# A four-layer graph network on one core: node blocks handed to the next layer while edge sums still run, four-step windows, node sums on TensorE

## The chip, the cores and the metric

The kernel runs on 1 core of one Trainium2 chip. The metric is device time in microseconds (us), and the time of a kernel is the median of its runs. A separate execution was taken with the hardware profiler; its own time is given beside the span of its trace.

## The reference

There are 6250 nodes with 128 features, 100000 edges sorted by destination, and four layers. Each layer gives a new value per node that is added to x and normalised over its 128 features. What each layer computes, cut to the sums over edges:

```
# layer 0, two rounds: attention with self loops (h = x @ W_node + b first)
g = h @ W;  e = leaky_relu((g*a_src).sum(-1)[src] + (g*a_dst).sum(-1)[dst], 0.2)
ex = exp(e - segment_max(e, dst)[dst])
h = segment_sum(g[src] * (ex / segment_sum(ex, dst)[dst]), dst) + bias
# layer 1: convolution with weights and degrees (deg: sums of weights plus 1)
out = segment_sum((x @ W)[src] * dis[src] * w * dis[dst], dst) + b
# layer 2: messages from x[src], edge type and time; 8-head attention over dst
message = x[src] * rel_emb * sigmoid(relu([x[src], rel_emb, time] @ W1 + b1) @ W2 + b2)
scores = ((x[dst] @ Wq + bq) * (message @ Wk + bk)).sum per head / 4
out = segment_sum((message @ Wv + bv) * softmax over dst (scores), dst)
# layer 3: gated recurrent update from summed messages
agg = segment_sum((h @ W_msg)[src], dst);  out = GRU(agg, h) @ W_out.T + b_out
# after each layer
x = layernorm(x + out)
```

The destinations are drawn as the square of a uniform number times 6250, so low node numbers have many more edges than high ones.

## The kernel before

The nodes are 49 blocks of 128, taken in 13 batches of up to 4 blocks (GROUPS). The edges are cut so that each of 832 steps (K) holds at most 128 edges that all go to one block. The steps follow the blocks in order, so the sums of low blocks are complete while later steps are still running.

The program is a row of stages. Where the text says "edge stage", the 832 steps are run in groups of 16 (U). For one step an indirect DMA issued by GpSimd (gather, L133) fetches the 128 source rows of a node table that the stage before has written to DRAM. A 128x128 matrix of zeros and ones (sel, written once to DRAM by the first stage and read back by SyncE in groups of 1 MB) says which row goes to which node of the block. One TensorE matmul adds sel-transposed times rows into PSUM (L415). The edge stages are attention 0 and 1 (attention_edges), the convolution and the messages of layer 3 (sum_edges), the scores of layer 2, and the weighted values of layer 2, which read rows that the scores stage has stored and so have no gathers.

The PSUM places are kept by the class Windows. A window is M = 8 steps. It opens three PSUM banks with three matmuls of zeros (L412), its eight steps add into places of 136 columns picked by a register, then one identity matmul adds what the first block of the window had before (L422), and ScalarE copies all nine places to the sums in SBUF, ACC (L431). The registers are loaded per group on TensorE and ScalarE.

An attention stage works in chunks of T = 64 steps, which is four groups. The destination terms are spread to the edges by matmuls with row selections (rsel, made on VectorE from dlrow, a row that a DMA spreads over the partitions, L382). When all 64 steps' rows are there, VectorE adds the last column of the gathered rows (L477, one operation per group), makes e (L479), scans for the running maximum over each destination (L485 to L505), and prepares shrink (L520, L522), which scales the sums of the chunk before. Only then are the rows scaled on ScalarE and summed. The gathered rows thus stay in their buffers (g, seven of one group in attention, eight in sum_edges) until that is done.

Between the edge stages lie node stages. They run over the 13 batches with all of the engines but GpSimd: they finish the sums (merged, or the lines after sum_edges), add to X (in SBUF for all 49 blocks), take means and variances on VectorE (stats), normalise everything when the last batch has its statistics (normalize, L342), and then make the next stage's table (for example attention_tables) and write it to DRAM. The next stage's gathers start when the table is written. After the last stage X is written to the output by two DMAs.

The order of instructions on each engine is set by a scheduler that follows the program's order and data[...].

Of the kernel before, what the change touches and what calls it, by code (L numbers as in the profile page):

```python
# [9 lines left out]
F32 = mybir.dt.float32  # L10
# [10 lines left out]
P = 128  # L21
# [13 lines left out]
M = 8  # L35
SB = 3
BANK = 512
SB_TOP = M // SB * BANK + M % SB * W
U = 16
T = 64  # L40
# [9 lines left out]
def kernel(ctx: ExitStack, tc: tile.TileContext, a: dict, out: bass.AP):  # L50
# [36 lines left out]
    Mt = table("mt", NP, D)  # L87

# [32 lines left out]
    MV = const.tile([P, NB, 2], F32, name="MV")  # L121
    VE = const.tile([P, NB], F32, name="VE")
    RS = const.tile([P, NB], F32, name="RS")
    NEWTON = const.tile([P, NB], F32, name="NEWTON")
# [122 lines left out]


# [45 lines left out]
    Wx, bl = [], []  # L294
    for l in range(2):
        w = const.tile([D, 130], F32, name=f"Wx{l}")
        nc.sync.dma_start(w[:, 0:D], a["L0_gnn_lyr_W"][l])
        Wx.append(w)
        bl.append(load(f"bl{l}", row_bcast(a["L0_gnn_lyr_bias"][l], D), P, D))
    W1l = load("W1l", a["L1_gnn_W"], D, D)  # L300
    b1l = load("b1l", row_bcast(a["L1_gnn_b"], D), P, D)
# [10 lines left out]


    def transposed(work, psum, src, g, name):
        pt = psum.tile([P, B, P], F32, name="tr", bufs=2)
# [6 lines left out]
    def stats(work, t0, g):  # L322
        for t in range(t0, t0 + g):
            s6 = work.tile([P, 6], F32, name="s6")
            nc.vector.bn_stats(s6, X[:, t, :])
            nc.vector.bn_aggr(MV[:, t, :], s6)

    def inverse_root(r, v):

        nc.scalar.activation(r, v, AF.Sqrt)  # L330
        nc.vector.reciprocal(r, r)
        for _ in range(2):
            nc.vector.tensor_mul(NEWTON, r, r)
            nc.vector.tensor_mul(NEWTON, NEWTON, v)
            nc.vector.tensor_scalar(NEWTON, NEWTON, -0.5, 1.5, op0=OP.mult, op1=OP.add)
            nc.vector.tensor_mul(r, r, NEWTON)

    def normalize():
        nc.vector.tensor_scalar(VE, MV[:, :, 1], EPS, None, op0=OP.add)
        inverse_root(RS, VE)  # L340
        for t in range(NB):
            nc.vector.tensor_scalar(X[:, t, :], X[:, t, :], MV[:, t, 0:1], RS[:, t:t + 1],  # L342
                                    op0=OP.subtract, op1=OP.mult)

    def by_step(keep, work, psum, rows, name):
# [3 lines left out]
        for k0 in range(0, K, K // 2):  # L349
            pv = psum.tile([P, K // 2], F32, name="bs", bufs=1)  # L350
# [22 lines left out]
    def row_selections(work, k0, make=False, n=U):  # L373
# [3 lines left out]
        if make:  # L377
            for h in range(2):
                n = U * P // 2
                row = work.tile([P, n], BF16, name="dlrow")  # L380
# [7 lines left out]
    class Windows:  # L388
# [4 lines left out]
        def __init__(self, psum, k0):  # L393
# [752 lines left out]
```

## Time and profile before

| | |
|---|---|
| Timed, median of 3 | 8493.26 us (8485.22 to 8526.25) |
| Profiled execution | 6808.89 us, span of its trace 6807.1 us |
| Granted TensorE clock, mean | 0.678 |
| PE, PEld, DVE, ACT, POOL busy | 62%, 44%, 26%, 33%, 62% |

The profiled execution is 1684 us shorter than the timed runs.

The stages, read from GpSimd's gathers and the matmuls of the windows, in us from the span's start:

| stage | from | to |
|---|---|---|
| preparation, first node stage | 0 | 140 |
| attention 0 | 140 | 1186 |
| node stage | 1186 | 1304 |
| attention 1 | 1304 | 2354 |
| node stage | 2354 | 2495 |
| convolution | 2495 | 3534 |
| node stage, queries | 3534 | 3660 |
| scores of layer 2 | 3660 | 4896 |
| maxima joined | 4896 | 5015 |
| values of layer 2 | 5015 | 5554 |
| node stage | 5554 | 5640 |
| messages of layer 3 | 5640 | 6678 |
| gates, output | 6678 | 6807 |

The costliest groups of instructions on the page (columns: line, engine, operation, tiles, count, then busy us and mean ns of one, then idle time before them):

```profile
L415 PE MATMUL win<-g,sel 128*128 128x128 f32 (+2 forms) x6656 | 1710.9, 412 | 747.8 <-issue 250.8
L133 POOL DMA_INDIRECT g<-g,SRCT x1664 | 1578.6, 949 | 722.2 <-issue 492.9
L431 ACT COPY ACC<-win 128x1224 f32 x520 | 610.9, 1175 | 1992.4 <-PE win L422 1745.2
L412 PE MATMUL win<-zero 1*128 1x512 bf16 x1560 | 618.0, 495 | 32.4 <-ACT ACC L431 27.6
L422 PE MATMUL win<-ACC,ident 128*128 x982 | 270.8, 371 | 157.9 <-ACT ACC L431 157.8
```

A float32 matmul runs as two passes, so 6656 passes in the first row are the 3328 steps of four stages. In the slices of the page GpSimd's row shows 7 in the stages with gathers, which is 0.94 us of each 1.25 us; the slices of less mark the node stages between them and the value stage.

### The profile page before, as it was taken

The page shows a single profiled execution, that of the slowest core. Times are in us where ns is not written, and L with a number is a line of the kernel's source. Part 1 is how long each engine was busy: PE and PEld are TensorE (multiplying, and loading weights), DVE is VectorE, ACT ScalarE, POOL GpSimd, SP SyncE. Part 2 cuts the span into 40 slices and gives each one's busy share as a digit, 9 for nine tenths or more (in the row PEclk, how much of TensorE's full clock was granted, in tenths as well). Part 3 has the DMA queues.
Part 4 walks back from the last instruction along what each step waited for, and adds up shares of the span by engine and source line. Part 5 has one row for each costly group of instructions (what it writes and reads, how often), then busy time and mean ns, then how long its engine had stood idle before and what let it go on. Part 6 is the DMA issues. An engine that isn't in the chain of part 4 may idle for free. (4 is left out here: it accounts for less than half of the span.)

```text
span 6807.1 us, 75064 instructions
## 1 busy us (share of the span) xinstructions
PE 4236.0 (62%) x21755; PEld 2971.6 (44%) x21755; DVE 1797.6 (26%) x4328; ACT 2223.4 (33%) x5686; POOL 4198.3 (62%) x4384
## 2 busy tenths in 40 slices
PE   3355554434454546666656888888867756767676
PEld 2244433333343434444434556555545544444443
DVE  4122222300000040000017777777730030000005
ACT  1243333233333323444434444455412221111112
POOL 1777777277777627777753666666524426777771
PEclk9566666666556665555557989999968875555557
DMA  4455555344444333333336888899746634333331
GB/s 121 142 159 153 160 166 146 106 125 122 129 134 141 107 93 108 103 108 102 109 86 189 238 239 245 245 260 261 228 144 203 207 103 125 103 108 102 109 102 32
DMA packets 736418, 997.90 MB, mean 147 GB/s; under 512 B 151184, under 2 KB 593352, under 8 KB 702744
## 3 DMA queue, kind: packets, MB, share of 16 engines
q1 hardware_dynamic: 587410, 662.03, 30.3%
q0 software_dynamic: 146992, 331.03, 19.3%
q8 instruction: 197, 3.23, 0.2%
q14 instruction: 197, 1.61, 0.1%
q10 hardware_dynamic: 1622, 0.01, 0.0%
HBM read 824.55 MB, written 168.09 MB: 146 GB/s over the span
## 5 line engine op out<-in xcount | busy, mean ns | idle before, releaser
L415 PE MATMUL win<-g,sel 128*128 128x128 f32 (+2 forms) x6656 | 1710.9, 412 | 747.8 <-issue 250.8
L133 POOL DMA_INDIRECT g<-g,SRCT x1664 | 1578.6, 949 | 722.2 <-issue 492.9
L415 PEld LDWEIGHTS win<-g,sel 128*128 128x128 f32 x6656 | 1348.1, 288 | 1246.1 <-issue 457.3
L431 ACT COPY ACC<-win 128x1224 f32 x520 | 610.9, 1175 | 1992.4 <-PE win L422 1745.2
L133 POOL DMA_INDIRECT xa<-xat,SRCT x832 | 823.2, 989 | 538.8 <-issue 319.4
L133 POOL DMA_INDIRECT g<-yt,SRCT x832 | 785.0, 943 | 394.5 <-issue 388.1
L133 POOL DMA_INDIRECT g<-mt,SRCT x832 | 785.1, 944 | 355.0 <-issue 246.8
L412 PE MATMUL win<-zero 1*128 1x512 bf16 x1560 | 618.0, 495 | 32.4 <-ACT ACC L431 27.6
L549 ACT ACTIVATE g<-g,EWT 128x128 f32<-128x128 f32 x832 | 318.5, 399 | 608.8 <-DMA g<-yt,SRCT 607.3
L532 ACT ACTIVATE g<-g 128x128 f32<-128x128 f32 x1664 | 516.5, 390 | 0.0
L835 PE MATMUL pk<-Wkv,mT 128*128 128x256 f32 x1664 | 461.0, 409 | 32.3 <-ACT mT L828 22.7
L952 POOL TENSOR_TENSOR vx<-v,exh 128x512 f32<-128x512 f32 x208 | 217.7, 1062 | 424.4 <-PE win L415 268.2
L422 PE MATMUL win<-ACC,ident 128*128 x982 | 270.8, 371 | 157.9 <-ACT ACC L431 157.8
L415 PE MATMUL win<-vx,sel 128*128 128x136 f32 x1664 | 281.4, 337 | 124.2 <-issue 118.1
L835 PEld LDWEIGHTS pk<-Wkv,mT 128*128 128x128 f32 x1664 | 300.8, 199 | 95.4 <-ACT mT L828 53.8
L840 ACT COPY kv<-pk 128x512 f32<-128x512 f32 x416 | 242.2, 589 | 302.1 <-issue 187.9
L415 PEld LDWEIGHTS win<-vx,sel 128*128 128x128 f32 x1664 | 265.7, 242 | 155.7 <-issue 145.4
L477 DVE TENSOR_TENSOR de<-de,g 128x16 f32<-128x16 f32 x104 | 17.2, 184 | 1093.9 <-DMA g<-g,SRCT 1093.9
L422 PEld LDWEIGHTS win<-ACC,ident 128*128 128x128 f32 x982 | 221.6, 277 | 170.1 <-ACT ACC L431 170.1
L1029 DVE SCALAR_TENSOR_TENSOR n<-pn,bhh,gate 128x512 f32<-128x512 f32 (+1 forms) x13 | 9.4, 720 | 1053.5 <-ACT gate L1021 1053.0
L483 PE MATMUL pch<-ident,e 128*64 128x128 f32 x26 | 10.8, 416 | 443.6 <-DVE e L479 443.6
L814 ACT ACTIVATE z<-rp,TMT 128x128 f32<-128x128 f32 x832 | 238.2, 374 | 145.5 <-DVE msg L811 143.5
(329 smaller groups left out, 4878.0 us busy)
## 6 DMA issues: line engine op xcount, KB each, us to landing
sel<-seld SPq DMA_DIRECT2D x208, 1024.0 KB
qb<-qt SPq DMA_DIRECT2D x832, 102.0 KB
seld<-sel SPq DMA_DIRECT2D x52, 1024.0 KB
vt<-kv SPq DMA_DIRECT2D x208, 256.0 KB
v<-vt SPq DMA_DIRECT2D x208, 256.0 KB
g<-g,SRCT POOLq DMA_INDIRECT x1664
dlrow<-dlr SPq DMA_DIRECT2D x104, 256.0 KB
rseld<-rsel SPq DMA_DIRECT2D x52, 512.0 KB
```

Of the source, the lines that this page charges most:

```text
L133: nc.gpsimd.indirect_dma_start(out=dst_tile, out_offset=None, in_=tab, in_offset=bass.IndirectOffsetOnAxis(ap=idx, axis=0))
L412: nc.tensor.matmul(self.win[:, i, :], zero[:, 0:P], zero, start=True, stop=False, skip_group_check=True)
L415: nc.tensor.matmul(flat_[:, ds(self.at[q], n)], sel, rows, start=False, stop=False, skip_group_check=True)
L422: nc.tensor.matmul(self.win[:, 0, 0:n], ident, ACCF[:, ds(before, n)], start=False, stop=True, skip_group_check=True)
L431: nc.scalar.copy(ACCF[:, ds(self.to[w], (M + 1) * W)].rearrange("p (b w) -> p b w", b=SB), self.win[:, :, 0:SB * W])
L477: nc.vector.tensor_add(de[:, i * U:(i + 1) * U], de[:, i * U:(i + 1) * U], g[:, :, D])
L532: nc.scalar.activation(g[:, q, 0:D], g[:, q, 0:D], AF.Copy, scale=g[:, q, D:D + 1])
L549: nc.scalar.activation(g[:, q, :], g[:, q, :], AF.Copy, scale=EWT[:, k0 + q:k0 + q + 1])
L814: nc.scalar.activation(z[:, q, :], rp[:, q, D:], AF.Copy, scale=TMT[:, k0 + q:k0 + q + 1])
L835: nc.tensor.matmul(pk[:, q - q0, :], mT[:, q, :], Wkv, start=True, stop=True)
L840: nc.scalar.copy(kv[:, q0:q0 + 2, :], pk)
L952: nc.gpsimd.tensor_mul(vx[:, :, 0:D].rearrange("p q (h d) -> p q h d", h=HD), v.rearrange("p q (h d) -> p q h d", h=HD), exh[:, u0:u0 + B, ...
```

## The change

Four parts belong together. First, a class Ahead takes the node work as a generator per batch. After every window's copy it is asked once (tick); when the step count has passed the batch's entry in EARLY, the batch starts, and each following window lets it go one step further. So eleven of the thirteen batches are issued between the windows of the edge stage before them. EARLY is a fixed list; whether the sums were complete by these steps is found from the edges in the preparation and kept in a register, late. After the last window (finish) the eleven batches are done again inside an If on late, with X read back from a copy in DRAM (XS); then the last two batches are issued, in turn. This holds for the five places between edge stages and for the end of the program, where each batch writes its rows of the output.

Second, the sums over nodes go to TensorE: diagonal matrices (dg, made by VectorE) scale blocks, a row of ones adds biases, the identity adds X. Means and variances are taken from PSUM per batch (norms), the inverse root is made by bit shift and three Newton steps (power), and ScalarE normalises. The layer's gate input h goes through DRAM (HTt).

Third, a window has M = 4 steps and two banks (NBK) instead of 8 and three.

Fourth, the chunks of attention are twelve of 64 steps and then 32, 16 and 16, instead of thirteen of 64.

With this the pools are opened once for several stages: the g buffers are 5 instead of 7 and 8, the work buffers of sum_edges 2 instead of 3, dlrow has 1 instead of 2, and the PSUM banks of node work ("na", "nb") are single. Some weights are loaded in the preparation, and GpSimd sets ACC to zero.

```diff
-M = 8
+M = 4
 SB = 3
+NBK = M // SB + 1
-T = 64
+CHUNKS = [64] * 12 + [32, 16, 16]
+T = max(CHUNKS)
+EARLY = [236, 332, 408, 472, 528, 580, 628, 672, 712, 756, 792]
...
+        lates = pp.tile([1, NE], F32, name="lates")
+        for j, k in enumerate(EARLY):
+            nc.vector.tensor_scalar(lates[:, j:j + 1], bkrow[0:1, k:k + 1], (j + 1) * B - 0.5, None, op0=OP.is_lt)
...
+    class Ahead:
+        def __init__(self, batch):
+            self.batch, self.j, self.on = batch, 0, None
+        def tick(self, k):
+            if self.on is None and self.j < NE and k >= EARLY[self.j]:
+                self.on = self.batch(*GROUPS[self.j])
+                self.j += 1
+            if self.on is not None and next(self.on, self) is self:
+                self.on = None
+        def finish(self, again=None):
+            while self.on is not None or self.j < NE:
+                self.tick(K)
+            with tc.If(late > 0):
+                if again is not None:
+                    nc.sync.dma_start(X[:, 0:NE * B, :], again)
+                for j in range(NE):
+                    for _ in self.batch(*GROUPS[j]):
+                        pass
+            rest = [self.batch(*g) for g in GROUPS[NE:]]
+            while rest:
+                rest = [r for r in rest if next(r, self) is not self]
...
-                row = work.tile([P, n], BF16, name="dlrow")
+                row = work.tile([P, n], BF16, name="dlrow", bufs=1)
...
-                nc.scalar.copy(ACCF[:, ds(self.to[w], (M + 1) * W)].rearrange("p (b w) -> p b w", b=SB),
+                nc.scalar.copy(ACCF[:, ds(self.to[w], NBK * SB * W)].rearrange("p (b w) -> p b w", b=NBK),
                                self.win[:, :, 0:SB * W])
+                if self.ahead is not None:
+                    self.ahead.tick(self.k0 + q + 1)
...
-            rows = es.enter_context(tc.tile_pool(name=f"ar{l}", bufs=7))
+        rows = es.enter_context(tc.tile_pool(name="ar", bufs=5))
...
+        def to_second(t0, g):
+            cc = merge_factors(node, SD[0], t0, g)
+            nc.vector.tensor_scalar(DEG[:, t0:t0 + g], ACC[:, t0:t0 + g, D + 2], 1.0, None, op0=OP.add)
+            own = own_rows(node, Gt[0], t0, g)
+            yield
+            dg = diagonals(node, (cc[:, 0], cc[:, 1]), g, 2)
+            yield
+            ph = batch_of(bank())
+            for q in range(g):
+                nc.tensor.matmul(ph[:, q, :], ACC[:, t0 + q, 0:D], dg[:, q, 0, :], start=True, stop=False)
+                nc.tensor.matmul(ph[:, q, :], own[:, q, :], dg[:, q, 1, :], start=False, stop=True)
+            hT = node.tile([P, B, P], F32, name="hT")
+            nc.scalar.activation(hT[:, :g], ph[:, :g], AF.Identity, bias=bl0, scale=1.0)
+            yield
+            attention_tables(node, bank, 1, hT, t0, g, SD[1])
+        ahead = Ahead(to_second)
+        attention_edges(0, work, rows, psum, D3, NV3, ahead)
+        ahead.finish()
...
```

The other batches (to_convolution, to_queries, to_messages, to_output) are built in the same way, with the normalisation between:

```diff
+    def norms(work, rows, g):
+        s6 = work.tile([P, B, 6], F32, name="s6")
+        mv = work.tile([P, B, 2], F32, name="mv")
+        rs = work.tile([P, 4, B], F32, name="rs")
+        for q in range(g):
+            nc.vector.bn_stats(s6[:, q, :], rows[:, q, :])
+            nc.vector.bn_aggr(mv[:, q, :], s6[:, q, :])
+        v, r, m, tmp = (rs[:, i, :g] for i in range(4))
+        nc.vector.tensor_scalar(v, mv[:, :g, 1], EPS, None, op0=OP.add)
+        power(r, v, tmp)
+        nc.vector.scalar_tensor_tensor(m, mv[:, :g, 0], -1.0, r, op0=OP.mult, op1=OP.mult)
+        return r, m
+    def normalized(to, rows, r, m, g):
+        for q in range(g):
+            nc.scalar.activation(to[:, q, :], rows[:, q, :], AF.Identity, bias=m[:, q:q + 1], scale=r[:, q:q + 1])
+    def add_rows(to, g, bias, t0, first=True):
+        nc.tensor.matmul(to[:, :g], ones[0:1, :], bias[:, None, :].to_broadcast([1, g, D]), start=first,
+                         stop=False, skip_group_check=True)
+        nc.tensor.matmul(to[:, :g], ident, X[:, t0:t0 + g, :], start=False, stop=False, skip_group_check=True)
```

## The prediction

> **What bounds the kernel now.** I read the page's slices first, then busy time cut by stage, then GpSimd's timeline at the stage borders, then VectorE's timeline inside the two attention stages, then the chain of waits in the value stage. Busy time by stage (columns: stretch, its length, then busy us and instruction count of PE, PEld, DVE, ACT, POOL, the granted clock, DMA share, GB/s):
>
> ```profile
> 140.00:1186.00 1046.00, 519.14 (x3828) 398.94 (x3827) 217.73 (x432) 357.63 (x1017) 792.46 (x832) 0.61 0.53 155
> 1186.00:1304.00 118.00, 66.44 (x324) 53.58 (x324) 54.97 (x104) 44.81 (x110) 0.00 (x0) 0.66 0.28 83
> 1304.00:2354.00 1050.00, 470.60 (x2956) 362.33 (x2956) 60.71 (x266) 352.31 (x971) 785.96 (x832) 0.60 0.44 129
> 5015.00:5554.00 539.00, 387.10 (x2183) 316.56 (x2182) 33.46 (x59) 148.48 (x310) 217.74 (x208) 0.82 0.63 200
> 6678.00:6807.00 129.00, 89.33 (x311) 45.99 (x310) 89.09 (x248) 36.23 (x56) 0.00 (x0) 0.83 0.10 26
> ```
>
> Five stages (attention 0, attention 1, convolution, scores, messages) each issue 832 gathers. GpSimd takes 0.94 us for one and 0.30 us to the next, 1.25 us, so 832 make 1040 us, the length of these stages; only the scores stage is longer (1236). GpSimd is the bound there, and stands still between stages:
>
> ```profile
> 1304.45 0.94 POOL L133 DMA_INDIRECT g<-g,SRCT  x1 [118.64 <-DVE bsv L352]
> 2495.43 0.94 POOL L133 DMA_INDIRECT g<-yt,SRCT  x1 [141.25 <-issue]
> 3659.81 0.95 POOL L133 DMA_INDIRECT xa<-xat,SRCT  x1 [126.17 <-issue]
> 5639.58 0.98 POOL L133 DMA_INDIRECT g<-mt,SRCT  x1 [101.82 <-DMA mt<-mt]
> ```
>
> The brackets are node work on the end's path. Of the last one 86 us lie after the value stage (5554 to 5640); behind the last gather come 129 us more.
>
> In the attention stages the gathered rows are held until the chunk's scores are known. VectorE near the end of a chunk in attention 0 (last gather done at 1105.5) and attention 1 (last gather at 1715.0):
>
> ```profile
> 1109.36 0.21 DVE L479 SCALAR_TENSOR_TENSOR e<-de 128x64 f32<-128x64 f32 x1
> 1109.49 0.88 DVE L382 TENSOR_SCALAR rsel<-dlrow,relid 128x1024 bf16<-128x1024 bf16 x2
> 1116.88 0.49 DVE L382 TENSOR_SCALAR rsel<-dlrow,relid 128x1024 bf16<-128x1024 bf16 x1 [4.71 <-DMA dlrow<-dlr]
> 1117.28 0.14 DVE L502 COPY cin<-pch 64x2 f32<-64x2 f32 x1
> 1127.98 2.29 DVE L368 TENSOR_TENSOR sel<-pdn,DLT 128x2048 f32<-128x2048 f32 x1 [7.70 <-PE win L415]
> ```
>
> ```profile
> 1736.72 0.18 DVE L477 TENSOR_TENSOR de<-de,g 128x16 f32<-128x16 f32 x1 [9.69 <-DMA g<-g,SRCT]
> 1756.59 0.19 DVE L477 TENSOR_TENSOR de<-de,g 128x16 f32<-128x16 f32 x1 [19.68 <-DMA g<-g,SRCT]
> 1756.69 0.15 DVE L520 SCALAR_TENSOR_TENSOR fac<-pch,OH 128x1 f32<-128x1 f32 x1
> 1756.88 0.35 DVE L522 SCALAR_TENSOR_TENSOR shrink<-ident,fac 128x128 f32<-128x128 f32 x1
> ```
>
> In attention 0 the first 16-gather buffer comes free 22.5 us after the chunk's last gather; a reload of dlrow stands inside that chain. In attention 1 fac and shrink queue behind adds that wait for the next chunk's gathers, and the first buffer is free after 46.5 us. Neither stops GpSimd, since seven buffers give it 3x20 us of lead. The value stage has no gathers; its chain runs through TensorE:
>
> ```profile
> 5213.15 3.81 issue
> 5216.97 3.97 PE win L415 x16
> 5224.01 1.19 ACT ACC L431
> 5225.24 0.80 PE win L412 x3
> ```
>
> Two groups of 16 steps take 20.5 us there: 10.25 us each, 52 times.
>
> **What the Trainium skill says.** "Perfetto Trace Analysis", Optimization Strategy: kernels with several regimes may gain by interleaving them, and a gap that repeats on the engine that should be saturated can mean too few buffers. The trace agrees with the first (118 to 141 us of idle GpSimd between stages); of the second it has none yet. "TensorE: Matmul & The Clock Gate", Architectural detail: VectorE and ScalarE queues are strict FIFO; the trace agrees, shrink waits behind an add it does not need for 30 us. The same page, Part 1: TensorE runs at half clock after an idle window; the trace agrees, 16 passes take 3.97 us after the 3.81 us pause and 2.05 to 2.09 later. "DMA: Bandwidth & Descriptors", Issuing engines are not separate DMA queues: all transfers share 16 engines; the trace agrees as far as dlrow lands 5 to 7 us after issue behind a 1 MB and a 512 KB write.
>
> **Part 1, node batches ahead.** Eleven of thirteen batches leave the stage borders; what stays is the last chunk, the flag and two interleaved batches. Attention 0 to 1: the last chunk has 16 steps instead of 64, first matmul 15.7 us after the gather, released by 22.5; then two batches of four steps: 28 small VectorE operations at 0.16 (4.5), four 128x512 products at 0.67 (2.7), TensorE and the copies about 8, the table's write and its landing about 4, the flag 2 (the sorting branch near the start costs VectorE 1.5); 21 to 22. So 118.6 becomes 45. The gathers also cease to wait for bsv. With norms (a batch: eight bn operations, 15 small ones, transposes, one more product) attention 1 to convolution becomes 22 + 30 = 52 for 141.3. Convolution to scores: window end 8, seven steps 36, = 44 for 126.2. Value to messages 27 for 86. Tail: window end 7, batches 25, output 4, = 36 for 129. Sum: -74 -89 -82 -59 -93 = **-397** (340 to 450, from 30% either way on what stays).
>
> **Part 2, buffers.** Pools are now shared, and the g buffers fall from seven (eight) to five, dlrow from two to one. A 64-step chunk fills four; the lead is one buffer, 16 gathers, 20 us. Any first release later than 20 us stops GpSimd, once per full chunk.
> Attention 0: 22.5 us already. In the changed program's VectorE order four rsel halves, not three of which two were ready, stand between e and cin, each after its own reload of the only dlrow. One such reload costs 4.7 us above, two in a row could be 5 to 12 more. I take 31: 11 us x 11 chunks = **+121** (60 to 165).
> Attention 1: one add that waits for the next chunk's first 16 gathers stands ahead of cin, ref, fac and shrink. These gathers end at 20, land at 22; cin to shrink take 6, scaling and 16 steps 7 to 8: release at 36, stop 16 us x 12 = **+192** (150 to 215). Behind the waiting add stands all of VectorE, behind that ScalarE's exponentials and the matmuls.
> Convolution and messages hold no row longer than a group: 0.
>
> **Part 3, windows of four steps.** Per group of 16: 8 zero matmuls instead of 6 (0.27 each, +0.5), 4 identity adds instead of 2 (0.24 each, +0.5), 4 copies of 128x816 (estimate 0.84, from 1.18 for 1224 and 0.59 for 512) instead of 2 of 1.18, less waiting for them: window alone 10.25 to about 10.45, x52 = +12 in the value stage. In the gather stages TensorE is busy half the time, which covers it; without that cover it would be 4x52x0.8 = 170.
>
> **Part 4, batches inside stages.** Hidden under gathers in four stages (DVE busy 0 to 218 of 1040 us). In the value stage TensorE is the path: per batch about 5 us of 128x512 matmuls (0.86 each) and transposes, and 3 us where TensorE's queue stands at a matmul whose operand VectorE or ScalarE has not finished: 8 x 11 = **+88** (40 to 140); with part 3, **+100**. A batch also puts two to four transfers of 256 KB on SP's queue (own rows in, table, X copy or HT out), some waiting 1 to 3 us for ScalarE with the next selection read behind them. I cost them at nothing: a selection is read one group (20 us) or, in the value stage, two groups ahead. Without that cover it is 33 x 3 = 100 us, part of C. On GpSimd's queue no batch issues anything.
>
> **Part 5, first node stage.** Single PSUM banks instead of pairs: a batch of four blocks 5.2 us (transpose, copy, matmul, copy, tables in series) for 2.4, x13 = +36; weights and flag sum +2: **+38** (25 to 45). POOL's memset of the sums lies ahead of gathers, under node work: 0.
>
> Sum: -397 +121 +192 +100 +38 = **+54**, 6809 to 6863. The timed median is 8493, 1684 us above the profiled execution, and no view says where. I add the difference to the median: 8547, rounded **8540**. If the extra lay in the gathers (0.4 us each), attention 0's stops would shrink to about 80 and attention 1's not, since its add waits for gathers anyway: +13, near no change.
>
> **Rivals.**
> A, forecast: stops about as priced, chance 0.42, own range 8450 to 8650.
> B, borders win: the stops are half or none, because the release chain overlaps better than the order suggests. -397 +138 +80 = -180: **8310**, chance 0.33. For it: before shows no stop at all, borders are measured; against it: 20 us of lead and a first release at 22.5 in the best case.
> C, other end and worse: head-of-line waits in TensorE's queue. Each tick puts matmuls that wait for VectorE between windows; if these fall in a chunk's first 16 steps they lengthen the stop, and at half clock the value stage's batches cost 15 us. Decides if a batch costs over 12 us of path: +54 +8x11 in the value stage +5x22 in attention: +250, **8740**, chance 0.15. Against it: half of TensorE is idle.
> D, the flag is up: all batches are redone, 55 x 7 us = +385 above A, **8925**; chance 0.02. The destination list first leaves each group 6 to 9 steps before the due step, so I expect it down.
> E, halves cancel: stops at 60%: 8450, chance 0.08.
>
> What a measurement can tell from no change is 0.5%, 42 us. Faster: B, a little of E and A's lower edge, 0.35. Same: most of E and a quarter of A, 0.18. Slower: the rest, 0.47. The range leaves out half of B's lower side and C's upper: 8250 to 8770.
>
> **What would show it.** In the profile after: GpSimd idle before the first gather of each stage 45, 52, 44, 27 us, tail 36; inside attention 0 and 1 one idle of 8 to 16 us every 64 gathers, ended by a window matmul; value stage near 640 us; first gather near 178. It is wrong if no such idle shows, if the borders stay above 70 us, or if the value stage grows over 700.

## The result, and the profile after

The changed kernel takes 8851.74 us (median of 4 runs, 8843.91 to 8870.07) where the kernel before takes 8489.24 in the same comparison: a ratio of 1.0431, 95% interval 1.0391 to 1.0471, slower by 363 us. The forecast was 8540, range 8250 to 8770: the direction was right, the size was not, and the time lies outside the range.

The profiled execution of the changed kernel took 8870.07 us (span 8868.0) on the kind of chip of the timed runs. That of the kernel before, 6808.89, fits another kind. The chips of all runs fall into two kinds: on the first (chips 1 and 11) the kernel before takes 6802 to 6828 us, on the second (chips 2, 4 and 10, and that of the timed runs) 8319 to 8526. So the two profiles can't be subtracted from each other; the tables below compare within a kind. A run over 1.5% slower than the fastest of its kernel is left out of the ratios: two of six in e11, one of four in e7, two of four in e8.

Busy time by stage of the changed kernel (columns as before: stretch, length, busy us and count of PE, PEld, DVE, ACT, POOL, granted clock, DMA share, GB/s):

```profile
222.00:2031.00 1809.00, 819.82 (x4302) 579.36 (x4302) 253.63 (x598) 418.91 (x1142) 789.44 (x832) 0.56 0.32 90
2031.00:2148.00 117.00, 77.26 (x440) 58.52 (x439) 40.12 (x145) 40.26 (x104) 0.00 (x0) 0.62 0.28 94
2148.00:3641.00 1493.00, 752.59 (x3564) 516.92 (x3563) 132.73 (x623) 419.23 (x1122) 787.88 (x832) 0.56 0.33 93
3742.00:5049.00 1307.00, 747.87 (x2746) 508.91 (x2746) 63.81 (x254) 427.07 (x1052) 786.26 (x832) 0.55 0.30 90
7013.00:7491.00 478.00, 451.90 (x2626) 308.55 (x2626) 104.03 (x355) 232.27 (x463) 219.94 (x208) 0.98 0.75 238
8782.00:8868.00 86.00, 61.52 (x281) 38.05 (x281) 23.57 (x101) 26.96 (x44) 0.74 (x1) 0.80 0.18 53
```

GpSimd at the stage borders:

```profile
2148.05 0.94 POOL L139 DMA_INDIRECT g<-g,SRCT  x1 [117.62 <-DMA g<-gt]
3742.26 0.94 POOL L139 DMA_INDIRECT g<-yt,SRCT  x1 [101.46 <-DMA yt<-own]
5137.69 0.95 POOL L139 DMA_INDIRECT xa<-xat,SRCT  x1 [88.47 <-DVE qt L839]
```

VectorE near the end of a chunk in attention 0:

```profile
1040.67 0.49 DVE L464 TENSOR_SCALAR rsel<-dlrow,relid 128x1024 bf16<-128x1024 bf16 x1 [15.38 <-remote]
1051.02 0.21 DVE L560 SCALAR_TENSOR_TENSOR e<-de 128x64 f32<-128x64 f32 x1
1056.74 0.49 DVE L464 TENSOR_SCALAR rsel<-dlrow,relid 128x1024 bf16<-128x1024 bf16 x1 [4.12 <-DMA dlrow<-dlr]
1062.01 0.48 DVE L464 TENSOR_SCALAR rsel<-dlrow,relid 128x1024 bf16<-128x1024 bf16 x1 [4.36 <-DMA dlrow<-dlr]
1065.84 0.48 DVE L464 TENSOR_SCALAR rsel<-dlrow,relid 128x1024 bf16<-128x1024 bf16 x1 [3.30 <-DMA dlrow<-dlr]
1066.24 0.14 DVE L583 COPY cin<-pch 64x2 f32<-64x2 f32 x1
```

The gathers are as quick as before (0.94 us), and their number is the same, but attention 0 is 1809 us long for 1046 and the convolution 1307 for 1039: GpSimd stops inside stages. Four halves of rsel (one, at 1051.16, is not shown) stand between e and cin, as forecast; three of them wait for a reload of dlrow. What was not forecast is in the first line: an idle of 15 us that ends with "remote", which is what the profile writes where no event that it holds ended the wait. The borders are 118, 101, 88 us and the tail 86; I had forecast 45, 52, 44 and 36.

### The profile page after: what moved, and what is told of

Read it like the earlier page. It is cut to its first block, busy times and chain, and to the rows that moved or that the text cites. A ratio compares the mean times of both kernels' runs of the same rounds, so it can differ in the third digit from the quotient of the medians.

```text
span 8868.0 us, 82549 instructions
## 1 busy us (share of the span) xinstructions
PE 5247.6 (59%) x24524; PEld 3548.2 (40%) x24524; DVE 1820.5 (21%) x5123; ACT 2520.6 (28%) x6417; POOL 4210.1 (47%) x4387
## 5 line engine op out<-in xcount | busy, mean ns | idle before, releaser
L513 ACT COPY ACC<-win 128x816 f32 x1040 | 870.5, 837 | 3038.5 <-remote 1926.9
L497 PE MATMUL win<-g,sel 128*128 128x128 f32 (+2 forms) x6656 | 1587.1, 405 | 137.4 <-ACT g L627 44.6
L504 PE MATMUL win<-ACC,ident 128*128 x2014 | 584.7, 385 | 1331.5 <-ACT ACC L513 1202.7
L494 PE MATMUL win<-zero 1*128 1x512 bf16 x2080 | 904.0, 523 | 246.9 <-ACT ACC L513 128.1
L504 PEld LDWEIGHTS win<-ACC,ident 128*128 128x128 f32 x2014 | 452.8, 276 | 1417.3 <-ACT ACC L513 1259.4
L957 PE MATMUL pk<-Wkv,mT 128*128 128x256 f32 x1664 | 601.4, 503 | 187.1 <-ACT mT L950 163.5
L960 PE MATMUL pq<-qb,rsel 128*128 128x136 bf16 x2496 | 301.1, 255 | 18.6 <-issue 12.0
L494 PEld LDWEIGHTS <-zero 1*128 1x128 bf16 x2080 | 131.9, 100 | 441.8 <-issue 391.5
L930 PE MATMUL rp<-RT,oty 128*128 128x256 bf16 x832 | 258.6, 311 | 59.3 <-issue 22.6
L948 PE MATMUL tr<-ident,msg 128*128 128x128 f32 x832 | 171.1, 329 | 206.2 <-DVE msg L933 200.0
```

The lines of the kernel that those rows point to most:

```text
L494: nc.tensor.matmul(self.win[:, i, :], zero[:, 0:P], zero, start=True, stop=False, skip_group_check=True)
L497: nc.tensor.matmul(flat_[:, ds(self.at[q], n)], sel, rows, start=False, stop=False, skip_group_check=True)
L504: nc.tensor.matmul(self.win[:, 0, 0:n], ident, ACCF[:, ds(before, n)], start=False, stop=True, skip_group_check=True)
L513: nc.scalar.copy(ACCF[:, ds(self.to[w], NBK * SB * W)].rearrange("p (b w) -> p b w", b=NBK), self.win[:, :, 0:SB * W])
L930: nc.tensor.matmul(rp[:, q, :], oty[:, o:o + P], RT2, start=True, stop=False)
L957: nc.tensor.matmul(pk[:, q - q0, :], mT[:, q, :], Wkv, start=True, stop=True)
```

## The experiments

**The same two kernels on other chips.** e0 and e5 are the kernel before, e4, e9, e13 and e16 the changed kernel, all unedited.

> The kernel before, unchanged, for a second profile. The first profiled execution took 6809 us, the timed runs 8490. Theory TE (TensorE in the timed runs finishes late: its completions reach the other engines several us after their modelled end, as the profile of the changed kernel shows in about 250 window copies): if this profile is near 8490 us, gathers still take 0.94 us and 1.25 us apart, GpSimd stops of 3 to 15 us ended by window matmuls stand between them, and some hundred window copies start more than 1 us after their identity matmul (none did in the first profile). Theory GA (the gathers are slower in the timed runs): 8490 us with about 1.65 us from gather to gather and no late copies. If it comes at 6809 again, neither is told apart.

> The changed kernel, unchanged, on another chip if the draw gives one. Two chips have shown up: on one the kernel before takes 6810 to 6830 us in every run, on the other 8480 to 8530. Theory chip (the changed kernel was profiled on the slower one, its late TensorE completions are that chip's and not the change's): where before takes 6815, this takes 6700 to 6900 and shows no late copies; e3 gives the stages, attention 0 near 1274, attention 1 near 1284, convolution 1040, messages 1040. Theory change (the node batches' bursts on TensorE bring the late completions about): 7000 or more beside a before of 6815, with late copies in all gather stages. If before takes 8490 here: 8850 either way, and the profile of the next run decides.

> The kernel before once more, for its profile in case this call is on the slower chip: then theory chip expects 8490 us with late window copies in some hundreds and GpSimd stops in stages that had none. On the faster chip: 6815 again, nothing new.

> The changed kernel again, beside e10 on one chip. On the faster chip (before 6815): e3's stages with the borders at the values seen (120, 101, 88, 85): 222 + 1274 + 120 + 1284 + 101 + 1040 + 88 + 1190 + 650 + 1040 + 85 = 7094 if the batches cost nothing, which is +280; my forecast was +54. On the slower chip (before 8340): 8650.

> The changed kernel unchanged, on a chip where before takes about 6810 if this is such a one. The run with chunks 48, 16 took 6976 there, with stage borders of 88, 99, 46 us and a tail of 39. If late TensorE completions on the slower chips hold the borders open, the unchanged kernel shows about 45 and 40 for the convolution border and the tail (forecast 44 and 36), no stops in convolution and messages, and about 7000 us in all, 1.03 times before; the attention borders tell what the third short chunk costs (20 to 30 us each above 88 and 99 if it does). If the borders are made of the batches, all are as on the slower chips (118, 101, 88, 85) and the total near 7090.

> The changed kernel unchanged once more, since the last call met a chip where before takes 8348. If this chip is one where before takes about 6810: about 7000 us, conv border and tail about 45 and 40 (forecast 44 and 36), no stops in convolution and messages, stops of about 220 and 270 in attention 0 and 1, attention borders 90 to 120. If it is one where before takes 8350 to 8500: 1.04 times before and the borders 118 to 127, 101 to 120, 88 to 101, 82 to 92 as four times so far.

| run | changed kernel | before, same chip | ratio, 95% interval |
|---|---|---|---|
| e16, first kind | 6979.78 | 6810.57 | 1.0241 [1.0220, 1.0262] |
| e13, second kind | 8654.92 | 8347.57 | 1.0371 [1.0349, 1.0393] |
| e4, second kind | 8666.26 | 8340.8 | 1.0391 [1.0343, 1.0439] |
| e9, second kind | 8870.69 | 8514.69 | 1.0405 [1.0371, 1.0439] |

e0 gave 6812.26 and e5 8356.89. So one program takes 6812 us on one chip and 8357 on another, and the changed kernel loses 169 us on the first kind and 307 to 356 on the second (8654.92 - 8347.57; 8870.69 - 8514.69). By stages, in us, each from a profile on the same kind of chip (first kind: e16 less the first profile of the kernel before; second kind: e4 less e5, one chip). A stage with gathers runs from its first to its last gather; the value stage is counted from the first to the last multiplication on GpSimd.

| term | forecast | first kind | second kind |
|---|---|---|---|
| preparation, first node stage | +38 | +81 | +83 |
| attention 0 | +121 | +226 | +343 |
| its border | -74 | -26 | -20 |
| attention 1 | +192 | +262 | +186 |
| its border | -89 | -43 | -58 |
| convolution | 0 | +4 | +103 |
| its border | -82 | -78 | -108 |
| scores | 0 | -53 | -3 |
| value stage | +100 | -45 | -47 |
| maxima joined, border to messages | -59 | -51 | -51 |
| messages | 0 | +4 | -18 |
| tail | -93 | -90 | -126 |
| sum | +54 | +191 | +285 |

(The sums are those of single profiled executions, and rounded; e16's is the longest of its four runs.) The clock does not tell the kinds apart: the kernel before has a mean of 0.678 in the first profile and 0.658 in e5. What does, in the traces, is how long ScalarE waits before it copies a window. The convolution's groups in the profile of the changed kernel (line, engine, operation, then busy us and mean ns, then idle time before and its releasers):

```profile
L497 PE MATMUL win<-g,sel 128*128 128x128 f32 x1536 | 381.3, 417 | 82.7 <-ACT g L627 44.6 <-issue 27.2 <-ACT ACC L513 10.7
L513 ACT COPY ACC<-win 128x816 f32 x190 | 159.1, 837 | 763.4 <-remote 534.7 <-issue 103.9 <-PE win L504 89.2
```

and of e16, the same program on a chip of the first kind:

```profile
L497 PE MATMUL win<-g,sel 128*128 128x128 f32 x1648 | 390.8, 405 | 27.8 <-ACT g L627 26.2 <-issue 1.3
L513 ACT COPY ACC<-win 128x816 f32 x204 | 169.8, 832 | 76.0 <-PE win L504 73.2 <-ACT g L627 0.4 <-issue 0.3
```

One matmul pass and one copy take nearly the same time in both (417 and 405 ns, 837 and 832 ns). But ScalarE stands idle before the copies for 763 us instead of 76, 535 of it until "remote", and when the last gather is issued TensorE has done 1536 of 1664 passes instead of 1648. Over the whole trace, the copies before which ScalarE stands idle for over 1 us beyond the modelled end of their window's last matmul are 0 in the first profile of the kernel before and 11 in e16, but 176 in e5 and 245 in the changed kernel's. In the value stage, without gathers, there is no such difference (523 us before on the first kind, 518 on the second).

Slower gathers are not seen: GpSimd takes 0.94 us for one on both kinds, in the convolution their packets take 0.12 us on average in e5 as in the first profile, and the last packet ends 2.8 us after the last gather in both. Nor are all steps slower: in attention 0 of the kernel before the first 16 steps after shrink take 8 us on both kinds, the other 48 of a chunk about 38 us in the first profile and 74 in e5. Why these windows are late on the second kind is not settled.

**Windows of four steps alone** (e1 everywhere, e11 in the value stage only).

```diff
-M = 8
+M = 4
```

```diff
-                sums = Windows(psum, k0)
+                sums = Windows(psum, k0, M4)
```

> The kernel before with windows of 4 steps and two banks alone. Theory hidden (TensorE and ScalarE have room in the gather stages, as forecast): +12 us, only the value stage, 8500. Theory TE (TensorE paces the stages in the timed runs, so each extra zero matmul, identity add and wait for a copy counts): 520 more windows at 0.4 to 0.8 us, +200 to +400, near 8790, which would be most of the whole change's +362.

> The kernel before with one edit: in the value stage alone a window has four steps and two banks (a second table of register values for it; eight gather buffers become seven in the sum stages to make room, which the convolution and the messages showed no need of). If the pause of TensorE, and the half clock after it, is what the four-step windows remove, the value stage falls from about 520 to 400 us, nothing else moves, and the whole gains 120 us: ratio 0.986 on a chip where before takes 8350 to 8520, 0.982 where it takes 6815. The old account (more zero matmuls and copies, plus 12) gives 1.002.

e1: 6917.25 against 6817.51, ratio 1.0144 [1.0127, 1.0161]; e11: 6692.45 against 6809.55, ratio 0.9821 [0.9805, 0.9836], 1.8% below the kernel before. (e11 has seven gather buffers instead of eight in the sum stages as well; none of its other stages moves by more than 9 us.) In both the value stage falls from 523 to 399 us. The chain of waits of e11 there (start, us, what):

```profile
5200.90 1.12 PE win L420 x8
5202.02 0.23 PE win L427 x2
5202.26 0.53 PE win L417 x2
5202.79 1.12 PE win L420 x8
```

A window is 8 passes at 0.14 us, its identity matmul and the next zeros, and no pause: four make 7.6 us where a group of 16 took 10.25. The kernel before paused 3.81 us once in two groups and ran 16 passes in 3.97 us after it. The clock granted in this stage is 0.99 in e11 for 0.82. "TensorE: Matmul & The Clock Gate" of the Trainium skill, Part 1, says that TensorE's clock is halved after an idle window and is full again after sustained work. This trace agrees: 16 passes take 3.97 us after the pause, and without a pause 8 take 1.12.

In attention 1 the same edit cost 145 us in e1, and the borders behind attention 0 and 1 grew by 48 and 39. In attention 1 VectorE's order is another one: shrink waits behind the third addition of the next chunk, where before it waits behind the second (1756.59 in the forecast's lines). e1's timeline at a chunk's end:

```profile
1863.41 0.21 DVE L478 TENSOR_TENSOR de<-de,g 128x16 f32<-128x16 f32 x1 [17.73 <-DMA g<-g,SRCT]
1883.42 0.19 DVE L478 TENSOR_TENSOR de<-de,g 128x16 f32<-128x16 f32 x1 [18.11 <-DMA g<-g,SRCT]
1883.71 0.35 DVE L523 SCALAR_TENSOR_TENSOR shrink<-ident,fac 128x128 f32<-128x128 f32 x1
```

The first buffer comes free 72 us after the chunk's last gather instead of 46, and the lead of three buffers is 60.

**Buffers alone** (e2: the kernel before with the changed kernel's buffers).

```diff
-            rows = es.enter_context(tc.tile_pool(name=f"ar{l}", bufs=7))
+            rows = es.enter_context(tc.tile_pool(name=f"ar{l}", bufs=5))
```

(The sum stages' rows likewise from 8 to 5, their work buffers from 3 to 2, dlrow from 2 to 1.)

> The kernel before with five g buffers instead of seven and eight, work buffers of sum_edges 2 instead of 3, dlrow 1 instead of 2; all else as before. Theory buffers (as forecast: the lead of one buffer is shorter than the first release): +300 us, 8790, GpSimd stops of 10 to 45 us once per 64 gathers in both attention stages, none in the convolution and message stages. Theory TE alone: what bounds the stages is TensorE's rate, a deeper lead only moves the stops: under +60, below 8550.

6991.82, ratio 1.0254 [1.0237, 1.0272]. Attention 0 grows by 112 us in twelve stops of 5 to 12 us at gathers 80, 144, 208 and so on, attention 1 by 123, the convolution and the messages by nothing. The lead of one buffer was read rightly; its price is 112 in attention 0, where I had 121, and 123 in attention 1, where I had 192. The scores stage is 52 us shorter here as well, though no line of it was edited, and in e3 (1189 us), which has no batches in it; e16's -53 is therefore not the batches' doing, and its cause stays open.

**Batches at the end** (e3, e10: all eleven batches after the last window; the same computation).

```diff
-EARLY = [236, 332, 408, 472, 528, 580, 628, 672, 712, 756, 792]
+EARLY = [832] * 11
```

> The changed kernel with EARLY = [832] * 11, so that no node batch is issued before the last window of its stage; all batches run one after the other behind it. Borders grow by 11 batches of 15 to 20 us each, five times: +800 to +1100 in all. What is to be read is the stages between first and last gather. Theory buffers: attention 0 (1809 us), attention 1 (1493), convolution (1307) and messages (1243) stay within 5%. Theory batches (node work between the windows delays TensorE): each of the four is shorter by 100 us or more, and the values stage falls from about 650 to 540.

> e3 again beside e9 on one chip, to price the batches between the windows. Theory batches: attention 0 at least 100 us shorter here than in e9, attention 1 and the convolution 50 or more, values 70 to 90. Theory hidden (gathers cover node work): within 20 us in the gather stages, values still 70 to 90 shorter.

e3, first kind: 7754.57; e10, second kind: 9498.45; one execution each. On the first kind the borders become 184, 264, 261 us and the tail 243, so moving the batches inside gives 774 us back (7754.57 - 6979.78). Inside the stages they cost nothing in attention 0 (1274 us in e3, 1272 in e16), the convolution (1040, 1042) and the messages (1040, 1042), and 28 us in attention 1 (1284, 1312), where e16 has 16 stops for 12. In the value stage, without cover, 396 against 478: 81 us, where 88 was forecast. On the second kind the cover is thinner (e9 less e10): convolution +114, messages +42, attention +7 and +5. The first node stage, which the batches don't touch, is 222 in e3 as in every run of the changed kernel. ScalarE there:

```profile
149.99 0.69 ACT L720 ACTIVATE hT<-nb,bn 128x512 f32<-128x512 f32 x1 [2.17 <-PE nb L718]
152.84 0.59 ACT L649 COPY gt<-nb 128x512 f32<-128x512 f32 x1 [2.16 <-PE nb L645]
155.96 0.59 ACT L354 COPY hT<-na 128x512 f32<-128x512 f32 x1 [2.53 <-PE na L352]
158.71 0.69 ACT L720 ACTIVATE hT<-nb,bn 128x512 f32<-128x512 f32 x1 [2.17 <-PE nb L718]
```

A batch takes 8.73 us (158.71 - 149.99): three times TensorE, then ScalarE, each waiting for the other. In the kernel before, with pairs of banks, twelve batches follow 2.4 us apart (first profile, 103.42 to 132.70).

**Order on VectorE** (e6, e14): de and shrink in one buffer, so that the next chunk's addition can't go ahead of shrink.

```diff
-                de = work.tile([P, T], F32, name="de")[:, 0:T_]
+                both = work.tile([P, T + P], F32, name="both", bufs=1)
+                de, shrink = both[:, 0:T_], both[:, T:]
```

> The changed kernel with de and shrink of a chunk in one tile, so that VectorE cannot take the next chunk's first add before shrink is made; all sums as before. Theory order (in attention 1 the first release waits for the next chunk's first 16 gathers, some 35 us, where the chain alone takes 20 to 23): stops in attention 1 fall from about 20 us per chunk to 3 to 6, -170 to -200 us against e4; attention 0, whose order is not touched, stays. Theory lead (five buffers are too few whatever the order): under -50.

> The changed kernel with de and shrink in one buffer, so that the next chunk's first addition can't go ahead of shrink on VectorE; before it ran on a chip with late TensorE completions and attention 1 lost only 44 us. Where completions come on time, the order alone should set attention 1: my forecast's release at 36 us falls to about 20, the stops of 269 us fall to under 80 (a gain of 190). If five buffers are too few whatever the order, the stops stay above 150.

8601.73 (ratio 1.0336 [1.0256, 1.0416]) and 8646.61 (1.0364 [1.0322, 1.0405]), both on the second kind. Attention 1 is 44 and 41 us shorter, not the 170 to 200 expected, and e14 is within 9 us of e13, its unedited companion. On this kind of chip the order is not what sets attention 1; on the first kind it wasn't tried.

**Buffers given back** (e7: order, six buffers for rows, dlrow in two, and single gt, own, fw, ref). The kernels run as e15 and e17 do not hold what their expectations describe: against the changed kernel, e15 has one edit, dlrow in two buffers, and e17 has that and the chunks 48, 16; neither has the order or the sixth buffer.

```diff
-                row = work.tile([P, n], BF16, name="dlrow", bufs=1)
+                row = work.tile([P, n], BF16, name="dlrow", bufs=2)
```

> As e6, and with six g buffers instead of five and two dlrow instead of one (paid for by single buffers of gt, own, fw, ref). Theory lead: with 40 us of lead no chunk stops GpSimd, both attention stages come to 1045 to 1060, another -230 us against e6, together -420 against e4, which would be clearly below before. Theory TensorE (node work and four-step windows pace the stages): attention 0 stays above 1200.

> As the run before it, with six buffers for gathered rows and dlrow in two buffers again (room from single gt, own, fw, ref). Where completions come on time a lead of two buffers, 40 us, covers both releases: stops in attention 0 fall from 220 us to under 20, in attention 1 under 20, and the whole goes under 6560 us, 0.96 of before, the change's own promise without its buffer cost. If attention 0 keeps more than 80 us of stops, the reload of dlrow or the node batches set its chain.

e7: 8560.78, ratio 1.0254 [1.0193, 1.0315]; e15: 8562.37, ratio 1.0264 [1.0241, 1.0287]. Attention 0 falls by 88 and 89 us in the two. All that e7 gained in attention 0 is thus in the one edit of e15; the sixth buffer shows no gain on the second kind.

**Fewer short chunks** (e12; e17 with dlrow in two as well).

```diff
-CHUNKS = [64] * 12 + [32, 16, 16]
+CHUNKS = [64] * 12 + [48, 16]
```

> The changed kernel with the attention chunks at the end 48, 16 instead of 32, 16, 16; nothing else. If the attention 0 to 1 border stays at 118 to 127 us because three short chunks pass through one chain of waits after the last gather, about 25 to 30 us each, one chunk less shortens it to about 92 to 100, and the attention 1 border from 101 to about 75; the whole gains 40 to 60 us (0.5 to 0.7%) against the changed kernel. If the border is made of the node batches and the landing of the table instead, both borders stay within 8 us of 120 and 101, as those of the convolution and the messages (88, 85 to 92) must in either case.

> The changed kernel with one buffer for de and shrink, six buffers for gathered rows, dlrow in two, and chunks 48, 16 at the end. Where completions come on time: stops of attention 0 and 1 from about 220 and 270 to under 40 together, borders 88 and 99 or less, about 6530 us, 0.96 of before. Where they come late: 8562 from this kernel with chunks 32, 16, 16, less 25 for each attention border if three short chunks queue up there: about 8515, 1.02 times before, borders about 95 and 76; unchanged borders (120, 100) say that the chunks are not the cause there.

e12: 6976.44, ratio 1.0245 [1.0229, 1.0261], the same as e16; its borders are 88, 99, 46 us, tail 39, where e16 has 93, 98, 48 and 39. So one chunk less is not worth 25 us a border, and my expectation fell. What the border is made of is seen in e16. ScalarE from the last gather (1493) to the next stage's first (1586):

```profile
1520.53 0.84 ACT L513 COPY ACC<-win 128x816 f32 x1 [3.19 <-PE win L504]
1550.94 0.84 ACT L513 COPY ACC<-win 128x816 f32 x1 [2.61 <-PE win L504]
1565.45 0.84 ACT L513 COPY ACC<-win 128x816 f32 x1 [1.01 <-PE win L504]
1581.77 0.27 ACT L649 COPY gt<-nb 128x128 f32<-128x128 f32 x1 [0.58 <-PE nb L645]
```

These are the last window copies of the chunks of 32, 16 and 16 and the last batch's table. The chunk of 32 is still being summed for 28 us after the last gather. The next chunk takes 30; its chain holds the reciprocal over all edges' terms, L638, 5.35 us, and its windows come 3.45 us apart (1.85 in the last chunk), at a granted clock of 0.50. The last takes 15, the batches 16, the table's landing 4. The chunk of 32 had its rows at 1452.6. VectorE took them up after the last copy of the chunk before, and then waited for dlrow twice more:

```profile
1467.42 0.83 ACT L513 COPY ACC<-win 128x816 f32 x1
1472.78 0.27 DVE L558 TENSOR_TENSOR de<-de,g 128x16 f32<-128x16 f32 x2
1488.62 0.48 DVE L464 TENSOR_SCALAR rsel<-dlrow,relid 128x1024 bf16<-128x1024 bf16 x1 [4.51 <-DMA dlrow<-dlr]
1489.02 0.14 DVE L583 COPY cin<-pch 32x2 f32<-32x2 f32 x1
```

So the chunks pass one after another, each through a chain of waits of its own. In e12 the sums end 67 us after the last gather, in e16 73, in the kernel before 61. Whether more buffers would mend it is not shown.

e17: 6905.59, ratio 1.0140 [1.0120, 1.0160], 1.4% above the kernel before. Against e12 attention 0 changes most, 1181 for 1264: the single dlrow costs 83 us on the first kind. Attention 1, which makes no rsel from dlrow, keeps its 1306.

**A version with three mends** (e8: the kernel before with four-step windows in the value stage alone, the small last chunks, one buffer for de and shrink).

> The kernel before with three things only: windows of 4 steps in the values stage alone, the small last chunks (32, 16, 16), and de and shrink in one tile (order on VectorE); 7 instead of 8 g buffers in sum_edges pay for the second offset table. No batches ahead. Theory parts (what helped in the whole change is four-step windows where TensorE is the bound, and short last chunks; the rest costs): values stage 522 to 398, -124; two borders at -35 to -45 each, -80; attention stages 1045 to 1050; sum -200, 6615 where before takes 6815, 8140 where before takes 8340. Theory tie (the order of the attention stages gets worse with the shorter chunks, or the values stage waits for its loads): above -80.

Four runs took 8396.67, 8420.97, 8699 and 8704 us against 8514.69, too far apart for a ratio. The trace (second kind) shows what the parts did: the value stage takes 400 us, but the borders behind attention 0 and 1 are 152 and 171 us, where e5, on another chip of that kind, has 147 and 159. At attention 0's last gather 1475 of 1664 passes are done, in e5 1472. So here the short chunks did not shorten the borders, though the seven buffers were kept. e11, with the first of these edits alone, is the version that stands.

**Inside an attention chunk.** e16's attention 1 from the end of a chunk's gathers to GpSimd's restart:

```profile
1888.39 0.18 DVE L558 TENSOR_TENSOR de<-de,g 128x16 f32<-128x16 f32 x1 [17.01 <-DMA g<-g,SRCT]
1891.13 0.35 DVE L603 SCALAR_TENSOR_TENSOR shrink<-ident,fac 128x128 f32<-128x128 f32 x1
1895.42 2.73 ACT L613 ACTIVATE g<-g 128x128 f32<-128x128 f32 x9
1898.06 0.81 ACT L513 COPY ACC<-win 128x816 f32 x1
1898.92 0.49 PE L504 MATMUL win<-ACC,ident 128*128 x2 [2.73 <-ACT ACC L513]
1902.87 0.84 ACT L513 COPY ACC<-win 128x816 f32 x1 [1.51 <-PE win L504]
1906.57 0.94 POOL L139 DMA_INDIRECT g<-g,SRCT  x1 [19.83 <-issue]
```

The addition that waits for the next chunk's gathers is where the forecast put it, and shrink follows 2.7 us later. But from shrink to the first free buffer it is 15.4 us, not 7 to 8. The first window's copy stands behind nine scalings of the next 16 rows in ScalarE's queue, the second window's identity matmul waits 2.73 us for that copy, and after this pause a window takes 3.4 us. The same place in e2, with as many buffers and windows of eight steps, takes 8.2 us:

```profile
1975.32 0.35 DVE L522 SCALAR_TENSOR_TENSOR shrink<-ident,fac 128x128 f32<-128x128 f32 x1
1983.49 0.95 POOL L133 DMA_INDIRECT g<-g,SRCT  x1 [11.25 <-PE win L415]
```

Over the twelve full chunks of attention 1, the median from shrink to the end of the 16th step is 7.4 us in e2, 14.7 in e16 and 14.4 in e3, which has no batches inside the stage; attention 0 has 7.8, 14.8 and 14.5, and 14.4 in e1, which differs from the kernel before (8.0) by the windows alone. So it is the four-step windows that lengthen the release, not the batches.

## Why the prediction was wrong, point by point

**What bounds it:** right on the first kind. In the attention stages GpSimd stops where the first buffer comes late, once in 64 gathers. On the second kind it stops elsewhere too (39 stops of over 1.5 us in attention 0 of the changed kernel's profile).

**The time it was added to:** the step that failed most for the timed result. "I add the difference to the median" took the 1684 us between the profiled and the timed executions as the same for both kernels. The runs show it to be the difference between two kinds of chip, and on the second the same change costs more: 169 us in e16, 307 to 356 in e13, e4 and e9. Of the 309 us by which the loss exceeds the forecast's 54 (363 - 54), 115 are already there on the first kind (169 - 54); the other 194 come with the second. Where they lie is known only from e4 and e5, a chip on which the change costs 325: more in attention 0 (+343 for +226), the convolution (+103 for +4) and the scores (-3 for -53), less in attention 1 (+186 for +262) and the tail. My remark on extra time in the gathers named the wrong place: the gathers are no slower, the copies of the windows are late; why stays open.

**The sum:** closer than its terms. On the first kind five terms lost 312 us more than forecast: attention 0 and 1 together 175, their borders 94, the first node stage 43. Two gains that I had not forecast hid most of it: 145 in the value stage, 53 in the scores. That the sum came within 137 us of the forecast there (191 - 54) is in part luck. Two smaller slips: I counted eleven stops in attention 0, where both attention stages have twelve, and E's stops at 60% give 8422, not 8450.

**Part 1, batches ahead:** on the first kind three of five borders nearly as forecast (convolution -78 for -82, value stage to messages -51 for -59, tail -90 for -93). Attention's were mis-sized: -26 and -43 for -74 and -89, and at 93 and 98 us they are above the 70 that I had named as a sign of being wrong. The failed step is "the last chunk has 16 steps instead of 64": 64 steps are unsummed at the last gather as before (1536 of 1664 passes are done in both), since the short chunks wait for each other; e16 shows 73 us for them behind attention 0 where I had 22.5, and 65 behind attention 1. The batches and the table's landing took 20 for the 21 to 22 of the sum.

**Part 2, buffers:** mechanism right, e2 confirms it apart (112 and 123). In the changed kernel the stops are 19 and 22 us a chunk on the first kind, for 11 and 16. The mis-sized term is the release after shrink: "scaling and 16 steps 7 to 8" holds with windows of eight steps (7.4 in e2) and is 14.7 with windows of four, some 7 us more in each of twelve chunks. In attention 0 a single dlrow costs 83 us (e17 less e12), about 7 a chunk, within the 5 to 12 that I gave it.

**Part 3, four-step windows:** wrong in both directions. "+12 in the value stage" is -124 (e11): I had counted the added instructions and not the pause that they do away with, although I showed the pause and the half clock after it. "TensorE is busy half the time, which covers it" fails in attention, where each chunk's first 16 steps lie on the chain that releases a buffer (above).

**Part 4, batches inside stages:** +81 in the value stage for +88, and on the first kind nothing in the gather stages but 28 us in attention 1: right in the main. On the second kind the convolution pays 114 (e9 less e10); there the cover that I took for given fails.

**Part 5, first node stage:** +81 for +38; a batch takes 8.73 us instead of the 5.2 estimated, as three TensorE and ScalarE steps take turns. No run has pairs of banks in the changed kernel, so the single banks are the likely reason and not a shown one.

**Rivals:** B (borders win) and E (shorter stops) were refuted by twelve stops a stage that are longer than forecast; D (the flag) did not occur, no batches are repeated in the borders. C comes nearest to the measured time (8740 with 8852), but its price, batches in TensorE's queue, is not what the runs show: in attention 0 and 1 they cost 7 and 5 us on the second kind (e9 less e10), 0 and 28 on the first, where C had 110.

## What to carry to other kernels

Price added small operations by what they do to the pauses around them, not only by their own length: the same four-step windows gain 124 us where they close a pause and lose 145 where the chain that releases a buffer grows longer. Handing node work to the next stage early pays what was forecast only where the last gather is followed at once by the last sum; in attention 64 steps still stood behind it. And before a profile's sum is added to a timed median, look whether both were taken at the same speed; here the gap of 25% was not an offset that stays the same for every kernel.

## What the runs showed of the hardware that was not expected

Chips differ by 22 to 25% for one program of this kind (6812 in e0, 8357 in e5, up to 8515 beside e9) at nearly the same granted clock (0.678 and 0.658 for the kernel before) and with gathers of 0.94 us on all. In e5 the window copies of the convolution wait for what the profile can't name:

```profile
ACT ACC L431 <- remote: 757.8, 42, 56.1
```

(us in total, times, longest): 42 waits, up to 56 us long, in a stage that has 8 buffers of rows and ran without a stop on the first kind; here it has 29 stops of over 2 us. That an attention stage with one buffer of lead has least room for such waits fits its growth on the second kind (+343 for +226 in attention 0), but attention 1 does not show it (+186 for +262).
